# Four layers of a hybrid network in one kernel: where the state-space scan of image 2 in layer 3 stands among the scans of layer 0

## The chip, the cores and the metric

The kernel runs on one core of a Trainium2 chip. TensorE (PE) multiplies matrices into PSUM; VectorE (DVE), ScalarE (ACT) and GpSimd (POOL) work element by element; SyncE (SP) issues almost all transfers. Each engine executes its own instructions in the order in which the program lists them. The metric is device time in microseconds (us) of one execution, the median of several runs.

## The reference, cut to what matters

Four images of 32 x 32 pixels and 256 channels pass four layers. Layer 0 is a convolution block with a selective scan, layer 1 a grouped convolution, layer 2 masked attention and a mixture of eight experts, layer 3 a second selective scan and a second mixture of eight experts. The scans are the only steps that run along the 1024 positions of an image one after the other:

```python
def step(h, inp):                        # layer 0: 512 channels, 64 states each
    xt, dtt, Bt, Ct = inp
    dA = jnp.exp(dtt[:, :, None] * A)
    h = dA * h + (dtt * xt)[:, :, None] * Bt[:, None, :]
    y = jnp.einsum('bdn,bn->bd', h, Ct)
    return (h, y)
...
def scan_step(h, inputs):                # layer 3: 512 channels, 16 states each
    x_t, dt_t, B_t, C_t = inputs
    A_bar = jnp.exp(dt_t[..., None] * A)
    B_bar = dt_t[..., None] * B_t[:, None, :]
    h_new = A_bar * h + B_bar * x_t[..., None]
    y_t = (h_new * C_t[:, None, :]).sum(axis=-1)
    return (h_new, y_t)
```

Everything that an image passes between the scans is per position or per image. The images don't depend on one another.

## The kernel before, in words

**A scan** is written (layer, image): (0, 3) is layer 0's of image 3. Its 512 channels are four blocks d of 128. A block is cut into *units*: a unit is a tile of 128 rows (channel and state) by 1024 positions. Layer 0 has 64 states, so 2 channels to a unit and 64 units to a block; layer 3 has 16 states, so 8 channels to a unit and 16 units to a block. Four scans of 256 and four of 64 units make 1280.

**A unit** (`scans`, L352 to L511) takes these steps. `load` (L419) fetches the step sizes of its channels, each channel's row broadcast over its states: one transfer (L425) per channel, so 2 of 256 KB in layer 0 and 8 of 64 KB in layer 3, all from SP. `decay` (L431) makes exp(dt A) on ACT. `first` (L441) spreads the inputs over the states on PE (`ps_rep`). Then DVE multiplies by B (L499) and runs the recurrence (L503, `TENSOR_TENSOR_SCAN`), POOL multiplies by C (L504), and after every second unit `pair` (L456) sums over the states on PE (`ps_y`); at the end of half a block the sum goes to DRAM (L479). Loads run four units ahead through five buffers, `ps_rep` has two. `chunk` (L372) fetches a block's inputs (`S`) and, with block 0, the scan's B and C (`rows`, two buffers each), 12 units ahead (AHEAD).

**The order of the units** is one list for the whole kernel, written by hand (L31): `SCANS = ((0, 0), (0, 1), (3, 0), (0, 2), (3, 1), (0, 3), (3, 2), (3, 3))`, each scan with all its blocks. Counted through from 0, (3, 1) is units 832 to 895, (0, 3) is 896 to 1151, (3, 2) is 1152 to 1215 and (3, 3) is 1216 to 1279.

**All other work** is twelve *stages* (L33), written as generators that yield between pieces and are laid between the steps of the units. `front` (image b) is layer 0 up to its scan. `middle` (b), L1782, is the rest of layer 0 (`back0`), layer 1, attention, the first experts and layer 3 up to its scan (`front3`); it asks for scan (0, b). `last` (b), L1792, is the rest of layer 3 (`back3`), the second experts and the output; it asks for scan (3, b). One stage is open at a time. `advance` (L526) runs the open stage's next piece. When none is open it takes the first stage in the list whose scan is whole, otherwise the first whose scan has its blocks 0 and 1; a stage that then comes to a block that isn't scanned yet waits, and no other is taken up meanwhile (L537).

**How much is laid beside a unit** is decided before anything runs, by an estimated clock for each engine (`Metered`, L92; `run`, L548): after each half of a unit, up to two pieces are laid down, as long as no engine's clock is ahead of DVE's. Where a scan's inputs aren't made yet by the time that its units are near (5 units, LATEST), `need` (L513) lays down stage pieces one after the other, with no units between them, until they are. Attention that is laid down in that way takes the scan's PSUM buffers for its scores (`ps_sx` in place of `ps_sc`, L1329).

Stages take SBUF from one stack, so a stage's transfers into its tiles wait until the stage before has let go of that memory.

Of the kernel before, what the change touches and what calls it, by code (L numbers as in the profile page):

```python
# [22 lines left out]
DC = DI // P  # L23
# [4 lines left out]
SCATTERS = ((0, 64), (64, 96), (96, 160), (160, 288), (288, 544))  # L28


SCANS = ((0, 0), (0, 1), (3, 0), (0, 2), (3, 1), (0, 3), (3, 2), (3, 3))  # L31

STAGES = (  # L33
    ("front", 0, None), ("front", 1, None), ("front", 2, None), ("front", 3, None), ("middle", 0, (0, 0)),
# [7 lines left out]
AHEAD = 12  # L42
LATEST = 5
# [89 lines left out]
class Hybrid:  # L133
# [182 lines left out]
    def scan_setup(self, stage, psum, name, n):  # L316
# [4 lines left out]
        nc, pool = self.nc, self.const  # L321
        G = P // n
        units = DI // G
        cols = pool.tile([P, units], F32, name="A_" + name)
        flat = self.a[name].rearrange("(u g) n -> u (g n)", g=G)
        for k in range(0, units, P):
# [6 lines left out]
        nc.vector.tensor_scalar(cols, cols, -1.0, None, ALU.mult)  # L333
        spread = pool.tile([3 * 32, 32 // G, P], BF16, name="spread_" + name)
        for s in range(3):
# [4 lines left out]
            )  # L340
        mine = stage.tile([P, G], F32, name="mine_" + name)
        nc.vector.tensor_reduce(
            mine, self.ident.rearrange("p (g n) -> p g n", n=n), AX.X, ALU.add
        )
        collect = pool.tile([P, 32 // G, 32], F32, name="collect_" + name)
        nc.gpsimd.memset(collect, 0.0)
# [4 lines left out]
    def scans(self, mp, psum):  # L351

        nc = self.nc
        units = []  # L360
        for scan in SCANS:
            G = P // self.states[scan[0]]
            units += [
                (scan, d, c, i, j)
                for d in range(DC) for c in range(2) for i in range(32 // G) for j in range(2)
            ]
        chunks, rows, waiting = {}, {}, []
        state = {}
        self.scan_psum = psum
        y = None  # L370

        def chunk(k):  # L372

            if k >= len(units):
                return
            scan, d, c, i, j = units[k]
            if (c, i, j) != (0, 0, 0):
                return
            n = self.states[scan[0]]
            self.need(scan, d)  # L380
            if d == 0:
                bct = self.mem["bc", *scan]
                pair = []
                for t in range(2):
                    x = mp.tile([P, L], F32, tag=f"rows{t}", name=f"rows{t}", bufs=2)
                    for g in range(P // n):
                        nc.sync.dma_start(x[g * n : (g + 1) * n, :], bct[t * n : (t + 1) * n, :])
                    pair.append(x)
                rows[scan] = pair
            S = mp.tile([3 * 32, 4, L], BF16, tag="S", name="S", bufs=2)  # L390
            for s in range(3):
                nc.sync.dma_start(
                    S[32 * s : 32 * s + 32, :, :],
                    self.mem["parts", *scan, d][s].rearrange("(j p) t -> p j t", p=32),
                )
            chunks[scan, d] = S

        def chunks_ahead(k, late=False):

            if not late and k + AHEAD < len(units) and units[k + AHEAD][2:] == (0, 0, 0):
                waiting.append(k + AHEAD)
            while waiting:
                scan, d = units[waiting[0]][:2]
                if ("parts", *scan, d) not in self.ready:
                    if waiting[0] - k > LATEST:
                        break
                    if not late:
                        return True  # L410
                    self.alone = True
                chunk(waiting.pop(0))
                self.alone = False
            return False

        def load(k):
            if k >= len(units):
                return
            scan, d, c, i, j = units[k]  # L419
            n = self.states[scan[0]]  # L420
            G = P // n
            a = mp.tile([P, L], F32, tag="dA", name="dA", bufs=5)
            for g in range(G):
                r = 64 * c + 32 * j + G * i + g
                nc.sync.dma_start(  # L425
                    a[g * n : (g + 1) * n, :],
                    self.mem["dt", *scan, d][r : r + 1, :].to_broadcast([n, L]),
                )
            state[k] = a

        def decay(k):  # L431
            if k >= len(units):
                return
            scan, d, c, i, j = units[k]
            G = P // self.states[scan[0]]
            col = (d * P + 64 * c + 32 * j) // G + i
            nc.scalar.activation(
                state[k], state[k], AF.Exp, scale=self.tables[scan[0]][0][:, col : col + 1]
            )

        def first(k):  # L441
            if k >= len(units):
                return
            scan, d, c, i, j = units[k]
            spread = self.tables[scan[0]][1]
            G = P // self.states[scan[0]]
            ps = psum.tile([P, L], F32, tag="x", name="ps_rep", bufs=2)
            for g in range(2):
                cols = slice(g * 512, (g + 1) * 512)
                nc.tensor.matmul(  # L450
                    ps[:, cols], lhsT=spread[:, i, :], rhs=chunks[scan, d][:, 2 * c + j, cols],
                    start=True, stop=True,
                )
            state[k] = (state[k], ps)

        def pair(k):  # L456

            nonlocal y
            scan, d, c, i, j = units[k]
            n = self.states[scan[0]]  # L460
            per = 32 * n // P
            collect = self.tables[scan[0]][2]
            if i == 0:
                y = psum.tile([P, 512], F32, tag="y", name="ps_y", bufs=1)
            h = [state.pop(k - 1), state.pop(k)]
            for g in range(2):
                for j in range(2):
                    at = 32 * (2 * g + j)
                    nc.tensor.matmul(
                        y[at : at + 32, :], lhsT=collect[:, i, :],  # L470
                        rhs=h[j][:, g * 512 : (g + 1) * 512],
                        start=(i == 0), stop=(i == per - 1), tile_position=(0, at),
                    )
            if i == per - 1:
                yo = mp.tile([P, 512], F32, tag="yo", name="yo", bufs=2)
                nc.scalar.copy(yo, y)
                to = self.keep(("y", *scan, d, c), [64, L])
                for g in range(2):
                    nc.sync.dma_start(to[:, g * 512 : (g + 1) * 512], yo[64 * g : 64 * g + 64, :])  # L479
                if c == 1:  # L480
                    self.done.add((scan, d))

        for k in range(AHEAD):
            chunk(k)
        for k in range(4):
            load(k)
        decay(0)
        decay(1)
        first(0)
        for k in range(len(units) + 4):  # L490
            waits = chunks_ahead(k)
            load(k + 4)
            if not waits:
                first(k + 1)
            decay(k + 2)
            if k < len(units):
                a, inp = state.pop(k)
                B, Cm = rows[units[k][0]]
                nc.vector.tensor_tensor(inp, inp, B, ALU.mult)  # L499
            yield  # L500
            if k < len(units):
                h = mp.tile([P, L], F32, tag="h", name="h", bufs=5)
                nc.vector.tensor_tensor_scan(h, a, inp, 0.0, ALU.mult, ALU.add)  # L503
                nc.gpsimd.tensor_tensor(h, h, Cm, ALU.mult)  # L504
                state[k] = h
            if k % 2 == 1 and 2 <= k < len(units) + 2:
                pair(k - 2)
            if waits:
                chunks_ahead(k, True)
                first(k + 1)  # L510
            yield  # L511
# [1332 lines left out]
```

## Time and profile before

| what | us |
|---|---|
| median of 3 runs (6766.81 to 6776.79) | 6769.17 |
| the profiled execution, by its own time | 6786.48 |
| span of the profiled execution, first to last instruction | 6784.8 |
| DVE busy (77% of the span) | 5227.3 |
| PE busy (79%) | 5361.8 |
| DVE, the recurrence: 1280 instructions, 2285 ns each | 2925.2 |
| DVE, the product with B: 1280 instructions, 1213 ns each | 1552.8 |

All times in what follows are from the span's start. The k-th `TENSOR_TENSOR_SCAN` on DVE is unit k, counted from 0, so the timeline of DVE gives the time of each unit. Those that matter here, by the start of the recurrence:

| unit | what begins there | us |
|---|---|---|
| 1028 | `last` of image 1, beside (0, 3) | 4798.9 |
| 1134 | `last` of image 1 is all laid down | 5236.8 |
| 1152 | (3, 2); with it `middle` of image 3 can go on | 5314.7 |
| 1211 | after it, `need` lays down most of the rest of `middle` of image 3 | 5598.8 |
| 1216 | (3, 3) | 6031.4 |
| 1222 | `last` of image 2, beside (3, 3) | 6060.5 |
| 1279 | the last unit | 6343.7 |

The profile's page has the whole execution's sums; the views by stretch of time, by tile and as a timeline show what happens in one stage. In a timeline a row gives start, length, engine, line, operation, output and inputs, how many instructions are merged, and in brackets the engine's idle time before and what ended it. Most instructions of the scans and stages have the line of the recording helper (L124), so they are told apart by tile.

### The profile page before, as it was taken

To read this page: it belongs to the slowest core of one execution; us is meant where nothing else is said; L and a number is where in the kernel's file an instruction comes from. 1 tells how busy PE (TensorE), PEld (TensorE's weight loads), DVE (VectorE), ACT (ScalarE), POOL (GpSimd) and SP (SyncE) were. 2 spreads that over 40 slices of the span, in tenths; PEclk is the share of its full clock that TensorE was granted. 3 is DMA by queue.
4 is the path that set the end of the run, shared out by engine and by line. 5 is a ranking of instruction groups with operands and counts; after the bars stand their busy time and mean duration, and the time that the engine had idled before them with its cause. 6 is when DMAs were issued, how large, how long until landed. Compare 5 with 4: busy or idle time off the path is not lost. (4 is left out here: it accounts for less than half of the span.)

```text
span 6784.8 us, 65796 instructions
## 1 busy us (share of the span) xinstructions
PE 5361.8 (79%) x20236; PEld 2166.3 (32%) x20320; DVE 5227.3 (77%) x4486; ACT 3447.1 (51%) x4112; POOL 3649.0 (54%) x1801
## 2 busy tenths in 40 slices
PE   6558778679798568979689679898698688967979
PEld 3002213122252022234145232253254222514556
DVE  8778998978798997789889987898899871247411
ACT  2426666445477334557558445476386344245411
POOL 0876786755457665555856655556756551054200
PEclk8559778589798578979789789898699788977989
DMA  2556665754365765446656755456666750146221
GB/s 73 147 144 160 179 171 155 193 133 124 102 164 158 185 162 143 116 117 178 180 148 170 184 149 132 107 140 176 177 167 171 167 133 14 50 130 151 79 62 35
DMA packets 394235, 937.44 MB, mean 138 GB/s; under 512 B 83220, under 2 KB 165728, under 8 KB 392224
## 3 DMA queue, kind: packets, MB, share of 16 engines
q1 hardware_dynamic: 391696, 930.53, 52.1%
q8 instruction: 172, 2.82, 0.2%
q0 software_dynamic: 2128, 2.13, 0.2%
q14 instruction: 239, 1.96, 0.1%
HBM read 842.59 MB, written 93.95 MB: 138 GB/s over the span
## 5 line engine op out<-in xcount | busy, mean ns | idle before, releaser
L124 POOL TENSOR_TENSOR h<-h,rows 128x1024 f32<-128x1024 f32 x1280 | 3031.3, 2371 | 1999.9 <-DVE h L124 1649.9
L124 DVE TENSOR_TENSOR_SCAN h<-dA,ps_rep 128x1024 f32<-128x1024 f32 x1280 | 2925.2, 2285 | 234.0 <-issue 106.0
L124 DVE TENSOR_TENSOR ps_rep<-ps_rep,rows 128x1024 f32<-128x1024 f32 x1280 | 1552.8, 1213 | 287.8 <-PE ps_rep L124 287.3
L124 ACT ACTIVATE dA<-dA,A_L_conv_A_log 128x1024 f32<-128x1024 f32 x1024 | 1154.2, 1145 | 727.6 <-DMA dA<-dt 636.5
L124 PE MATMUL ps_rep<-S,spread_L_conv_A_log 96*128 96x512 bf16 x2048 | 766.7, 465 | 740.7 <-DVE h L124 709.1
L124 PE MATMUL ps_y<-h,collect_L_conv_A_log 128*32 128x512 f32 x4096 | 804.1, 762 | 96.0 <-POOL h L124 94.6
L124 PE MATMUL ps_h<-xTm,we 128*128 128x512 f32 x1536 | 719.4, 608 | 3.4 <-ACT h_m L124 1.8
L124 PE MATMUL ps_e<-we,h_m 128*128 128x256 f32 x3072 | 703.2, 382 | 10.9 <-ACT h_m L124 10.4
L124 ACT ACT_TABLE_LOAD x495 | 635.1, 1283 | 76.2 <-PE ps_h L124 44.4
L124 PEld LDWEIGHTS <-spread_L_conv_A_log 96*128 96x128 bf16 x2048 | 161.6, 103 | 1520.5 <-DVE h L124 1209.6
L124 PEld LDWEIGHTS ps_e<-we,h_m 128*128 128x128 f32 x3072 | 583.3, 191 | 157.2 <-issue 45.4
L124 DVE SCALAR_TENSOR_TENSOR tb<-ps_e,cw,tb 128x256 f32<-128x256 f32 x512 | 220.7, 474 | 415.5 <-PE ps_e L124 415.5
L124 ACT ACTIVATE h_m<-ps_h,cols 128x512 f32<-128x512 f32 x384 | 260.4, 686 | 473.8 <-PE ps_h L124 471.0
L124 ACT ACTIVATE dA<-dA,A_L_attn_A_log 128x1024 f32<-128x1024 f32 x256 | 293.5, 1148 | 390.3 <-DMA dA<-dt 354.0
L124 ACT ACTIVATE p<-ps_sc 128x512 f32<-128x512 f32 x432 | 234.4, 594 | 450.6 <-PE ps_sc L124 295.5
L124 PEld LDWEIGHTS ps_h<-xTm,we 128*128 128x128 f32 x1536 | 292.9, 194 | 341.8 <-issue 295.2
L124 PE MATMUL ps_at<-p,v 128*32 128x512 f32 x1024 | 357.6, 616 | 45.8 <-ACT p L124 35.1
L124 PE MATMUL ps_rep<-S,spread_L_attn_A_log 96*128 96x512 bf16 x512 | 185.4, 451 | 205.8 <-DVE h L124 184.3
L124 PE MATMUL ps_sc<-qT,kT 32*128 32x512 f32 x864 | 251.7, 654 | 42.1 <-ACTq L1248 24.5
L124 PE MATMUL ps_at<-p,ones 128*32 128x512 f32 x1024 | 275.1, 616 | 0.0
L124 PEld LDWEIGHTS ps_y<-h,collect_L_conv_A_log 128*32 128x32 f32 x4096 | 107.9, 120 | 495.9 <-POOL h L124 248.3
L124 PE MATMUL ps_cv<-pad,diag 128*128 128x512 f32 x576 | 260.4, 594 | 0.0
(311 smaller groups left out, 5012.4 us busy)
## 6 DMA issues: line engine op xcount, KB each, us to landing
dA<-dt SPq DMA_DIRECT2D x2048, 256.0 KB
dA<-dt SPq DMA_DIRECT2D x2048, 64.0 KB
we<-in_L_ffn_W_dram SPq DMA_DIRECT2D x64, 512.0 KB
parts<-parts SPq DMA_DIRECT2D x64, 384.0 KB
S<-parts SPq DMA_DIRECT2D x96, 256.0 KB
dt<-sp_r SPq DMA_DIRECT2D x64, 256.0 KB
y<-yo SPq DMA_DIRECT2D x128, 128.0 KB
y_back<-y SPq DMA_DIRECT2D x64, 256.0 KB
```

The lines of the kernel that those rows point to most:

```text
L124: return got(*args, **kw)
```

## The change

`SCANS` becomes a list of scans with ranges of blocks, and may hold a pause:

```diff
-SCANS = ((0, 0), (0, 1), (3, 0), (0, 2), (3, 1), (0, 3), (3, 2), (3, 3))
+SCANS = (
+    ((0, 0), range(DC)), ((0, 1), range(DC)), ((3, 0), range(DC)), ((0, 2), range(DC)),
+    ((3, 1), range(DC)), ((0, 3), range(2)), ((3, 2), range(DC)), ((0, 3), range(2, DC)), None,
+    ((3, 3), range(DC)),
+)
...
         for scan in SCANS:
+            if scan is None:
+                units += [None] * (LATEST + 1)
+                continue
+            scan, blocks = scan
             G = P // self.states[scan[0]]
             units += [
                 (scan, d, c, i, j)
-                for d in range(DC) for c in range(2) for i in range(32 // G) for j in range(2)
+                for d in blocks for c in range(2) for i in range(32 // G) for j in range(2)
             ]
+
+        def some(k):
+            return k < len(units) and units[k] is not None
```

Every step of a unit (`chunk`, `load`, `decay`, `first`, the two products, the recurrence, `pair`) asks `some(k)` instead of `k < len(units)`. So units 0 to 1023 are what they were. Then come (3, 2) whole as units 1024 to 1087, (0, 3) blocks 2 and 3 as 1088 to 1215, six empty places that issue nothing for a unit but in which stages can be advanced, and (3, 3) as places 1222 to 1285.

What the stages do with that follows from `advance`. When `last` of image 1 is laid down, at unit 1134, (3, 2) is whole and (0, 3) isn't; so `last` of image 2 comes next, and `middle` of image 3 after it. In the order of the built kernel's instructions `last` of image 2 begins at unit 1134; by the pause all but its last 22 pieces are laid down; there the inputs of (3, 3) are missing, and `need` lays down those 22 pieces and then `middle` of image 3 up to the first parts of (3, 3), with no unit between them. The units of (3, 3) come next, the first ten of them beside the last pieces of `front3`. `last` of image 3 begins beside them, but its pieces wait for blocks of (3, 3). No instruction of the computation is added or taken away; the attention of image 3 takes its scores in `ps_sx` throughout.

More of the change, by code (lines that the diff above doesn't have):

```diff
@@ L372, in chunk @@
         def chunk(k):
-            if k >= len(units):
+            if not some(k):
                 return
@@ L398, in chunks_ahead @@
         def chunks_ahead(k, late=False):
-            if not late and k + AHEAD < len(units) and units[k + AHEAD][2:] == (0, 0, 0):
+            if not late and some(k + AHEAD) and units[k + AHEAD][2:] == (0, 0, 0):
                 waiting.append(k + AHEAD)
@@ L416, in load @@
         def load(k):
-            if k >= len(units):
+            if not some(k):
                 return
@@ L431, in decay @@
         def decay(k):
-            if k >= len(units):
+            if not some(k):
                 return
@@ L441, in first @@
         def first(k):
-            if k >= len(units):
+            if not some(k):
                 return
@@ L495, in scans @@
             decay(k + 2)
-            if k < len(units):
+            if some(k):
                 a, inp = state.pop(k)
@@ L500, in scans @@
             yield
-            if k < len(units):
+            if some(k):
                 h = mp.tile([P, L], F32, tag="h", name="h", bufs=5)
@@ L505, in scans @@
                 state[k] = h
-            if k % 2 == 1 and 2 <= k < len(units) + 2:
+            if k % 2 == 1 and 2 <= k < len(units) + 2 and some(k - 2):
                 pair(k - 2)
```

## The prediction

> **What bounds the kernel now.** I read the page first. DVE is busy 77% and PE 79%, and which of them holds depends on the stage. The chain that ended last reaches back only some 6% of the span, through PE's expert products, so the end is a stretch with PE alone. That made me cut the last 2000 us by the units' times (front) and ask for the busy time of each stretch: length, then PE, PE's weight loads, DVE, ACT, POOL, then the granted PE clock, the DMA share and GB/s.
>
> ```profile
> 4798.90:5236.80 437.90, 389.09 (x1540) 198.30 (x1540) 403.05 (x325) 298.35 (x290) 265.34 (x119) 0.89 0.63 165
> 5236.80:5314.70 77.90, 37.33 (x108) 4.36 (x108) 67.92 (x39) 19.52 (x17) 47.38 (x23) 0.50 0.89 224
> 5314.70:5598.80 284.10, 220.51 (x961) 82.47 (x969) 229.44 (x186) 122.25 (x160) 158.81 (x74) 0.84 0.58 140
> 5598.80:6014.60 415.80, 361.12 (x1381) 166.44 (x1388) 75.65 (x183) 150.72 (x212) 44.57 (x35) 0.91 0.11 36
> 6014.60:6060.50 45.90, 23.12 (x68) 4.59 (x68) 38.32 (x27) 22.60 (x29) 38.31 (x23) 0.57 0.72 182
> 6060.50:6346.00 285.50, 214.54 (x791) 105.20 (x792) 223.88 (x188) 147.78 (x151) 149.83 (x70) 0.78 0.63 157
> 6346.00:6477.30 131.30, 130.60 (x467) 87.16 (x465) 16.73 (x39) 25.82 (x37) 2.34 (x1) 1.00 0.09 27
> 6477.30:6784.80 307.50, 262.73 (x904) 176.91 (x904) 43.52 (x115) 53.34 (x82) 14.81 (x12) 0.89 0.18 53
> ```
>
> Row 1 is `last` of image 1 beside layer 0's units: both engines near 90%. Row 2 is 18 units with no stage beside them: PE half idle. Rows 3 to 5 are `middle` of image 3, first with the units of (3, 2), then (row 4) with none, then with the first units of (3, 3). Rows 6 and 7 are `last` of image 2, beside (3, 3) and then alone; row 8 is `last` of image 3. So there are three places where one kind of work runs without the other: row 2, row 4 and rows 7 and 8. From (0, 3) on, the order that nothing can cut is (0, 3), `middle` 3, (3, 3), `last` 3; the question is what stands beside it.
>
> Then the same view for tile dA alone, whose DVE count is recurrences, for 57 units from the start of each `last`, first layer 0's, then layer 3's:
>
> ```profile
> 4798.90:5045.00 246.10, 130.25 (x57) 63.37 (x57) 0.80 0.66 170
> 6060.50:6343.60 283.10, 130.25 (x57) 64.06 (x56) 0.77 0.63 156
> ```
>
> A unit takes 4.32 us in the first and 4.97 in the second, beside the same stage work. SP's timeline gives a reason, 48 issues (six units of layer 3) in one go:
>
> ```profile
> 6231.07 23.34 SPq L425 DMA_DIRECT2D dA<-dt  x48
> ```
>
> That is 0.486 us an issue, 3.9 us a unit, where DVE needs 3.60 (starts of recurrences in DVE's timeline, 3929.25, 3932.85, 3936.45).
>
> **The change part by part.** It adds no instruction; it moves what stands beside what. I follow it from unit 1024, with the profiled execution's times.
>
> 1. *Units 1024 to 1087 are (3, 2) in place of block 2 of (0, 3).* The stage work beside them is the same: the end of `middle` 2, then `last` 1 from unit 1028. Each unit now issues 8 transfers on SP in place of 2. By the two rows above, (283.1 - 246.1) x 64/57 = 41.5; I take **+40**. The bounds are 0 (SP at 3.9 us a unit keeps ahead of 4.32) and 42. Its 16 transfers of `rows` only move from before unit 1152 to before 1024, with loads four units ahead as cover; the buffers are free, since they were those of (3, 1).
>
> 2. *`last` 2 begins at unit 1134, beside (0, 3) blocks 2 and 3.* Row 2's **78 us** without a stage are filled: -78. `last` 2 then has 82 units of layer 0 beside it, as `last` 1 had. In `last` 1 the products `ps_e` of expert block 11, the first of the 22 pieces left, started at 5155.4, 356.5 us after unit 1028. The 22 pieces are three blocks of 16 `ps_h` and 32 `ps_e` and two halves; alone such a block takes 13.77 us (`ps_e` starts 6353.17 and 6366.95, in PE's timeline), so 3 x 13.77 + 2 x 6.9 = 55.1. `last` 2 takes 356.5 + 55.1 = 411.6 in place of rows 6 and 7, 416.8: **-5** (bounds -20 and +5).
>
> 3. *`middle` 3 runs with no unit beside it.* From 5314.7 to unit 1222 (rows 3 to 5) it took 745.8.
>  - 5314.7 to 5606.7, the end of its third pair of heads, with 60 units beside it: 292. Alone a pair of heads takes 22.7 (5606.67 to 5629.37 in PE's timeline), beside units 33.9: 3 x 11.2 = 34 saved. The normalisation between `ps_h` and `ps_tr` (5404 to 5429) takes 25, alone 8 to 9 (5897.7 to 5905.3, 7.6): 16. The wait before the first scores (5475 to 5505) takes 30, of which PE's last 11.2 are no unit's: I take 13, 17 saved. `ps_o` of `back0` 23, against 15.9 for 64 at 0.248 us (58 in 14.4 at the end): 7. Other products 6. Lost: the y and u of (0, 3) can only be fetched when `last` 2 lets go of its memory; `last` 3 shows that fetch, 6477.3 to the last block at 6504.9, 27.6, against 15.5 here (5314.7 to 5330.2): -13. Together 67 saved, 225 left.
>  - 5606.7 to 5973.4 is alone already: 366.7, unchanged.
>  - 5973.4 (the step sizes of (3, 3)) to 6060.5, 87: the first unit of (3, 3) now follows at once, without four units of (3, 2) before it (17 us) and six of (3, 3) counted here (29): 87 - 17 - 29 = 41, and I add 7 for the transfers of `rows`, `S` and `dt` of (3, 3), which landed behind those units: 48.
>  So 225 + 367 + 48 = 640, **-106**. Bounds: PE's own work in the first part is 227.9 less 40.9 (`ps_rep`) and 41.5 (`ps_y`), 145.5, and with the fetch some 160, which gives -171; if only the heads get faster, -60.
>
> 4. *(3, 3) has nothing beside it.* `last` 2 is gone, `last` 3 waits for it. What a lone scan costs isn't in the trace; DVE's pace is 3.60, SP's 3.9. SP also issues the stores of y, `S` and the fetches of `last` 3, some 0.3 us a unit, and each fetch of a block waits on SP for that block's store to land (store 6089.91, fetch 6095.40: 4.4 us after the store's issue had ended), with the loads of later units behind it. I take 4.3 us: 63 x 4.3 = **+271**. Bounds: 3.60 (227) and 4.97 (313). The first ten units share ACT and DVE with `front3`'s end, within that.
>
> 5. *`last` 3.* Before, its fetch came after `last` 2 (6477.3 to 6504.9), here three of four blocks are in before the scan ends. After the last recurrence: POOL, `ps_y`, copy 6.6 us (6343.66 to the store at 6350.21), store to fetch 5.5 as above, and some 5 for the load, then as before from the last gating to the end:
>
> ```profile
> 6504.92 2.48 POOL L124 TENSOR_TENSOR y_back<-y_back,gate_back 128x512 f32<-128x512 f32 x2 [1.36 <-DMA y_back<-y]
> 6506.24 14.40 PE L124 MATMUL ps_o<-w_L_attn_W_out,y_back 128*128 128x256 f32 x58 [2.62 <-POOL y_back L124]
> ```
>
>  6784.8 - 6504.9 = 279.9, with 17 before it 297 in place of 307.5: **-11**.
>
> Sum: 40 - 78 - 5 - 106 + 271 - 11 = **+111 us**, or 6897 for the profiled execution (6786.48). The median stands 17 us below that execution, so 6769.2 + 111 = **6880 us**. The change fills 78 us of DVE and buys `middle` 3 a free run; it pays with a whole scan in the open, which before stood under `last` 2.
>
> A rule against the change is in the Trainium skill, "DMA: Bandwidth & Descriptors", section "Measured (HBM→SBUF, 128 partitions, SWDGE, issued from GpSimd)": transfers below 64 KB are dominated by descriptors, and one of 64 KB takes 0.95 us. If the eight of a unit ran one after the other, 7.6 us a unit, an estimate from that page, (3, 3) would take 479 us and the sum would be +319. The trace speaks against it, with recurrences of layer 3 that start 3.8 us apart (3913.31 to 3940.05, seven steps): transfers overlap, and SP's issue is the limit.
>
> **The rivals.**
> - *Slower still.* The round trip of y on SP starves the lone scan (4.97 or more, as in its slowest row), and `middle` 3 is held by its own chain, not by the units (-60): 40 - 78 - 5 - 60 + 313 - 11 = +199, 6968. For it: PE is busy only 145 of 292 us there. Against it: heads are measured alone.
> - *A wash.* SP keeps ahead in (1), the lone scan runs at 3.75 (236) and `middle` 3 gives 145: 0 - 78 - 5 - 145 + 236 - 11 = -3, 6766.
> - *Faster.* The one mechanism is that units laid between a stage's pieces cost `middle` 3 more than their own time. It decides in 5314.7 to 5606.7: with the lone scan at DVE's 3.60 (227) and +40 kept, `middle` 3 must save 187 to be 14 us ahead, 147 with step 1 at nothing; so the first part must fall from 292 to some 144, below the bound of 160, or with the swap free to some 184. At its bound of -171 and the swap free: 0 - 78 - 5 - 171 + 227 - 11 = -38, 6731.
> - That the order isn't changed as said is excluded by the built program.
>
> **How the numbers follow.** Forecast, +50 to +160: 0.78. Slower still: 0.12. Wash: 0.05. Faster: 0.05. A measurement of this kernel tells 0.2%, 13.5 us, from no change. Faster 0.05, the same 0.05, slower 0.90. All bounds together run from -53 (0 - 78 - 20 - 171 + 227 - 11) to +211 (42 - 78 + 5 - 60 + 313 - 11), but they are independent; 8 in 10 lie from about +35 to +190: **6805 to 6960**.
>
> **What would show it.** Right: the 64 last recurrences stand in a stretch of about 270 us with PE mostly idle and a clock of 0.5; no recurrence for some 640 us before it; row 2's gap is gone; heads of 22.7 us all through. Wrong: the lone scan at 3.6 us a unit, step 1 free, or `middle` 3 below 560 us.

## The result and the profile after

| | before | after |
|---|---|---|
| median, both measured side by side (us) | 6772.98 (6766.81 to 6788.31) | 6871.71 (6861.00 to 6884.43) |
| the profiled execution (us) | 6786.48 | 6884.43 |
| its span (us) | 6784.8 | 6882.7 |
| PE's mean granted clock | 0.827 | 0.822 |

The change makes the kernel slower by 98.7 us, a ratio of 1.0143 with a 95% interval of 1.0118 to 1.0168. 6880 was forecast. The two spans lie 97.9 us apart, so the profiles can be cut against each other.

The page's sums hide it: PE is busy 5402.2 us in place of 5361.8, DVE 5222.2 in place of 5227.3. As before I read by stretches. The view is the busy time of stretches, for the kernel after, with the columns of the prediction's first table. The rows are `last` 1, `last` 2, `middle` 3 in three parts (to the end of its third pair of heads, to the step sizes of (3, 3), to the first unit of (3, 3)), the scan (3, 3), and `last` 3:

```profile
4813.97:5288.80 474.83, 394.69 (x1540) 201.36 (x1540) 403.78 (x326) 302.77 (x296) 265.45 (x119) 0.87 0.60 163
5288.80:5701.20 412.40, 363.85 (x1400) 192.85 (x1400) 321.02 (x274) 236.11 (x237) 208.25 (x95) 0.90 0.53 140
5701.20:5894.50 193.30, 149.73 (x655) 64.88 (x655) 32.60 (x71) 54.60 (x73) 21.98 (x18) 0.87 0.18 57
5894.50:6261.20 366.70, 329.29 (x1293) 153.46 (x1289) 64.92 (x170) 114.47 (x158) 18.77 (x15) 0.91 0.09 29
6261.20:6311.29 50.09, 28.50 (x61) 11.35 (x60) 8.82 (x12) 37.59 (x54) 27.24 (x22) 0.84 0.36 107
6311.29:6589.55 278.26, 130.47 (x380) 17.58 (x380) 219.55 (x131) 83.10 (x82) 168.89 (x81) 0.52 0.58 162
6589.55:6882.70 293.15, 265.22 (x912) 177.31 (x912) 45.04 (x114) 55.25 (x84) 8.45 (x6) 0.91 0.12 35
```

The row of 78 us without a stage is gone. In its place stands the sixth row: 278 us in which PE is busy for 130 and has a clock of 0.52. Between the start of the last unit of layer 0 (5640.0) and that of the first unit of (3, 3) lie 671 us, where the prediction's sign was some 640 without a recurrence: besides the 610 us of `middle` 3 they hold the last 61 of `last` 2, which the prediction had among its terms but not in that sign. Of the 610, DVE is busy for 106. `last` 1 beside its units takes 474.8 us, where before it took 437.9: that is the swap itself.

The same view for tile dA alone. The first row is the 57 units from unit 1028, most of them layer 3's now; the second is the scan (3, 3), 63 intervals:

```profile
4813.97:5097.40 283.43, 130.25 (x57) 64.02 (x56) 0.78 0.60 162
6311.29:6589.55 278.26, 144.04 (x63) 72.22 (x63) 0.52 0.58 162
```

283.4 us for 57 units is 4.97 each, to the hundredth the pace that layer 3's units had beside `last` before (283.1). Alone they take 4.42.

The end of the kernel, in the timeline, answers to the last lines of the prediction: the last gating comes 14 us after the start of the last recurrence (6589.55), where the prediction had 17, and with the products that follow it the rest runs as before.

```profile
6603.45 2.48 POOL L129 TENSOR_TENSOR y_back<-y_back,gate_back 128x512 f32<-128x512 f32 x2 [6.68 <-issue]
6604.77 15.12 PE L129 MATMUL ps_o<-w_L_attn_W_out,y_back 128*128 128x256 f32 x58 [5.61 <-POOL y_back L129]
```

Put beside the prediction's steps, from the same units or products in both profiles:

| step | predicted (us) | measured (us) |
|---|---|---|
| up to unit 1024 (same instructions) | 0 | 4798.4 - 4783.3 = +15.1 |
| 1: units 1024 to 1134 | +40 | 490.4 - 453.5 = +36.9 |
| 2: row 2 gone; `last` 2 | -78; -5 | -77.9; 412.4 - 416.8 = -4.4 |
| 3: `middle` 3 | -106 | 610.1 - 745.8 = -135.7 |
| 4: the scan (3, 3) alone | +271 | +278.3 |
| 5: `last` 3 | -11 | 293.15 - 307.50 = -14.4 |
| sum | +111 | +97.9 |

### The profile page after: what moved, and what is told of

Its sections match the earlier page's. It is cut to its first block, busy times and chain, and to the rows that moved or that the text cites. A ratio compares the mean times of both kernels' runs of the same rounds, so it can differ in the third digit from the quotient of the medians.

```text
span 6882.7 us, 65921 instructions
## 1 busy us (share of the span) xinstructions
PE 5402.2 (78%) x20320; PEld 2159.4 (31%) x20320; DVE 5222.2 (76%) x4486; ACT 3490.3 (51%) x4120; POOL 3648.7 (53%) x1801
## 5 line engine op out<-in xcount | busy, mean ns | idle before, releaser
L129 PE MATMUL ps_rep<-S,spread_L_attn_A_log 96*128 96x512 bf16 x512 | 204.4, 492 | 284.9 <-DVE h L129 259.7
L129 ACT ACTIVATE p<-ps_sc 128x512 f32<-128x512 f32 x384 | 208.3, 594 | 406.1 <-PE ps_sc L129 401.6
L129 PEld LDWEIGHTS ps_h<-xTm,we 128*128 128x128 f32 x1536 | 291.9, 194 | 344.9 <-issue 294.1
L129 PE MATMUL ps_sc<-qT,kT 32*128 32x512 f32 x768 | 223.8, 654 | 31.7 <-DMA dA<-dt 13.8
```

Of the source, the lines that this page charges most:

```text
L129: return got(*args, **kw)
```

## The experiments

Two things were to be tested: whether the change is slow for the reason given (a scan left in the open, worth more than `middle` 3's free run), and whether layer 3's pace, on which steps 1 and 4 rest, comes from SP's issues. The rival for the second was that the transfers land late for a reason of their own (their size, the rows they read, the DMA engines' load), or that ACT's queue holds the exps back.

The stretches of every run, from its profile, in us, each from the start of its first recurrence to the start of the first recurrence behind it; (3, 3) stands last and is counted as 63 intervals. In the kernels with the order before, and in e3, (3, 3) stands beside `last` 2. e3, e5, e8 and e9 were timed once, the others four times or more:

| kernel | time (us) | (3, 0) | (3, 1) | 1024-1087 | (3, 3) |
|---|---|---|---|---|---|
| before | 6773-6786 | 304.5 | 305.1 | 273.4 (layer 0) | 312.3 |
| after | 6871.7 | 308.2 | 307.8 | 310.6 | 278.3 |
| e1 after, one load of eight rows | 6932.6 | 338.1 | 330.4 | 320.9 | 264.3 |
| e2 before, the same load | 6869.6 | 334.3 | 333.7 | 274.6 (layer 0) | 320.9 |
| e3 after, `last` 2 behind `middle` 3 | 6943.1 | 307.5 | 305.9 | 311.1 | 305.9 |
| e4 before, pause | 6792.7 | 308.0 | 305.5 | 275.4 (layer 0) | 310.2 |
| e5 after, one load of one row | 6751.5 | 291.0 | 290.6 | 272.7 | 233.2 |
| e6 after, loads five ahead | 6830.7 | 296.1 | 299.2 | 307.1 | 277.2 |
| e7 after, late copy | 6881.8 | 311.9 | 315.8 | 308.6 | 279.3 |
| e8 after, y fetched from ACT | 6877.6 | 310.0 | 308.8 | 312.0 | 278.8 |
| e9 after, eight loads of one row | 6877.0 | 307.6 | 306.5 | 311.6 | 277.4 |
| e10 after, state by state | 6764.4 | 291.8 | 289.4 | 273.6 | 242.1 |
| e11 before, state by state | 6693.4 | 291.9 | 290.9 | 274.3 (layer 0) | 271.6 |
| e12 before, state by state, five ahead | 6697.0 | 290.2 | 290.3 | 274.3 (layer 0) | 271.0 |

### The order's own parts: e3 and e4

e3 lets `last` 2 open only after `middle` 3:

```diff
             can = [
                 x for d in (DC - 1, EARLY) for x in self.todo
-                if x[2] is None or (x[2], d) in self.done
+                if (x[2] is None or (x[2], d) in self.done)
+                and (x[:2] != ("last", 2) or all(z[0] != "middle" for z in self.todo))
             ]
```

> The changed order of units, but the stage last of image 2 may not open before middle of image 3 has: it then stands beside (3, 3) again, and units 1134 to 1215 have nothing beside them. Theory (what counts is which units have a stage beside them): 82 bare units of layer 0 at 3.9 us, 320 in place of 351; middle of image 3 as short as in the changed kernel; (3, 3) and last of image 2 together about 417 in place of 278 and 61 alone; in all 60 to 80 slower than the changed kernel, 6930 to 6960. Rival (stage work and units add up whatever their order, so only the place of (3, 2) counts): within 20 of 6872.

Measured: 6943.1 us, 71 above the changed kernel. The view is the busy time of stretches for this kernel: units 1134 to 1151, units 1152 to 1215, the time to the first unit of (3, 3), the scan (3, 3):

```profile
5284.00:5354.75 70.75, 37.31 (x108) 4.35 (x108) 64.66 (x38) 19.52 (x17) 47.33 (x23) 0.51 0.83 217
5354.75:5583.28 228.53, 125.33 (x380) 14.78 (x380) 216.05 (x128) 70.94 (x63) 149.14 (x64) 0.50 0.55 145
5583.28:6182.28 599.00, 507.94 (x1993) 228.87 (x2009) 103.90 (x250) 208.43 (x287) 67.43 (x53) 0.90 0.11 35
6182.28:6488.19 305.91, 214.91 (x775) 96.78 (x776) 245.00 (x201) 153.76 (x161) 174.57 (x85) 0.74 0.64 163
```

Now layer 0's last 82 units are bare (70.8 + 228.5 us, PE's clock 0.50) and (3, 3) stands under `last` 2 again, in 306 us. With (3, 2) moved ahead there is one `last` for two stretches, these 82 units and (3, 3): beside whichever it stands, the other is bare. That `last` 2 fills the gap in the changed kernel is part of what the change earns, as step 2 has it.

e4 has the order before, written in the new form, with the pause of six empty places ahead of (3, 3):

```diff
+SCANS = tuple(
+    (x, range(DC)) for x in ((0, 0), (0, 1), (3, 0), (0, 2), (3, 1), (0, 3), (3, 2))
+) + (None, ((3, 3), range(DC)))
```

> The order of the kernel before, with the six empty places ahead of (3, 3) and nothing else changed. Theory (the pause itself costs nothing): within 15 us of 6773; middle of image 3 has all 64 units of (3, 2) beside it in place of 60, and last of image 2 opens ten units into (3, 3) in place of six. Rival (the pause is a part of the loss, since no unit stands ready when the inputs of (3, 3) are made): 25 to 50 slower.

Measured: 6792.68 us, ratio to before 1.0015 (1.0003 to 1.0026). That is 8 us in a loss of 99: the pause is not what costs.

### One transfer in place of eight, and why it was slow: e1, e2, e5, e9

e1 and e2 load a unit of layer 3 with one transfer of 512 KB:

```diff
+            r = 64 * c + 32 * j + G * i
+            if scan[0] == 3:
                 nc.sync.dma_start(
...
+                    a,
+                    self.mem["dt", *scan, d][r : r + G, :].unsqueeze(1).to_broadcast([G, n, L]),
+                )
```

> The changed kernel, with the eight loads of a unit of layer 3 (64 KB each, one per channel) written as one transfer of 512 KB with the same rows. Theory (SP's issues set the pace of layer 3's units): the lone scan (3, 3), 278 us for 63 steps in the changed kernel, falls to 3.6 to 3.7 us a unit, about 230; units 1024 to 1134, 490 us there, fall by about 35 to the 454 of the kernel before; the other three scans of layer 3 gain 10 to 30 each; in all 90 to 150 us faster than the changed kernel, 6720 to 6780. Rival (the chain of landing, exp, recurrence and freed buffer sets the pace, or the bytes do): the lone scan stays at 4.2 to 4.5 us a unit or gets slower, and the time stays within 20 us of 6872.

> The kernel before with the same one load for a unit of layer 3. Theory (SP's issues): its layer-3 scans, 4.76 to 4.97 us a unit beside stages, come near the 4.1 to 4.3 of layer 0's units, 30 to 40 us for each of four: 6640 to 6690. The changed order stays slower than this by 40 to 100, because its scan (3, 3) still has nothing beside it. Rival (chain or bytes): 6773, no change.

Measured: e1 6932.6 us, 1.0222 of before (1.0202 to 1.0243), slower than the change itself; e2 6869.55, 1.0126 (1.0107 to 1.0145). Both expectations of the "issue" theory fell, and so did the rival's, by which the time would stay where it was. Only the lone scan gained (264.3, its undisturbed intervals 3.54 us), and beside stages all got worse. I had changed two things at once, as the next two runs were made to show. e5 loads one row, broadcast to all 128 partitions, in one transfer; e9 keeps eight transfers but lets all read one row:

```diff
+                r = 64 * c + 32 * j + G * i                              # e5
+                nc.sync.dma_start(a, self.mem["dt", *scan, d][r : r + 1, :].to_broadcast([P, L]))
...
-                r = 64 * c + 32 * j + G * i + g                          # e9
+                r = 64 * c + 32 * j + G * i + (g if G == 2 else 0)
```

> The changed kernel, but a unit of layer 3 loads one channel's row broadcast to all 128 rows in one transfer of 512 KB, in place of eight transfers of 64 KB from eight rows (the other seven channels' step sizes are left out, so those values are not the reference's). SP issues one instruction a unit, the bytes written are the same. Theory 'SP's issue is the limit': the lone scan of (3, 3) falls from 278 to about 240 us, units 1024 to 1087 from 311 to about 280, the whole from 6872 to 6760-6800. Theory 'a transfer of 512 KB lands as one piece and therefore later than eight of 64 KB': like the merged load from eight rows, 320 us for units 1024 to 1087, about 264 for the lone scan, 6920-6940 in all. Theory 'eight source rows in one transfer were what slowed the merged load': units 1024 to 1087 at or below 311, 6840-6870.

> The changed kernel with its eight transfers of 64 KB a unit of layer 3, but all eight read the same row (seven channels' step sizes are left out, so those values are not the reference's). It stands between the changed kernel (eight issues, eight rows) and the load of one row in one transfer (6751). Theory 'the eight issues a unit on SP': as the changed kernel, 308-313 us for units 1024 to 1087, 274-282 for the lone scan, 6865-6890 in all. Theory 'reading eight rows of DRAM': as the single row, 273 and 233, about 6750.

Measured: e5 6751.46 us, a little below what the "issue" theory had; e9 6877.04, as that theory had it. The busy time of units 1024 to 1087 in the kernel after (its lone scan is in the first table of this part):

```profile
4798.36:5108.99 310.63, 230.60 (x844) 108.37 (x845) 247.29 (x203) 162.31 (x167) 170.74 (x82) 0.78 0.61 167
```

The same two stretches (units 1024 to 1087, then (3, 3) alone), first e1, then e9, then e5:

```profile
4841.75:5162.65 320.90, 235.04 (x844) 108.55 (x845) 245.78 (x204) 161.02 (x166) 170.80 (x82) 0.75 0.65 159
6372.49:6636.74 264.25, 131.03 (x380) 17.28 (x380) 219.52 (x131) 83.12 (x82) 169.29 (x81) 0.51 0.60 170
```

```profile
4795.09:5106.67 311.58, 230.84 (x844) 109.15 (x845) 247.29 (x203) 162.41 (x167) 170.59 (x82) 0.77 0.67 166
6304.12:6581.56 277.44, 130.58 (x380) 17.58 (x380) 219.54 (x131) 83.09 (x82) 169.04 (x81) 0.52 0.64 163
```

```profile
4742.60:5015.31 272.71, 223.93 (x844) 106.81 (x845) 246.88 (x204) 162.46 (x168) 170.86 (x82) 0.82 0.62 189
6222.80:6456.05 233.25, 130.25 (x380) 17.25 (x380) 221.06 (x132) 82.08 (x82) 169.33 (x81) 0.51 0.59 191
```

All three do the same work on DVE, ACT and POOL (busy times within 2 us of each other). e9 is the changed kernel again: eight reads of one row are as slow as reads of eight rows. e5 is faster than the changed kernel by 38 and 45 us, and than e9, which reads the same one row, by 39 and 44: the number of transfers decides, not the rows they read. What then held e1? The trace also records every packet of the DMA engines. I counted how many were under way at once in units 1024 to 1087, as shares of the stretch:

| packets under way | after | e1 | e5 | e10 (below) |
|---|---|---|---|---|
| none | 13% | 4% | 26% | 19% |
| exactly 8 | 4% | 46% | 2% | 1% |
| 16 | 16% | 12% | 23% | 35% |

In e1 eight packets are under way for 46% of the stretch, and for 65% of a quiet piece of its lone scan: the transfer whose outermost count is 8 keeps eight at a time going. This agrees with the Trainium skill: "DMA: Bandwidth & Descriptors", section "Rules for kernel authors", has it that the engines of a transfer follow from the slowest dimension of its access patterns, so that one of fewer than 16 keeps the transfer to that many engines. The same section advises to merge many small transfers into one large; e1 shows that this alone can lose.

SP is not what is late in e1. The view is who SP waited for in units 1024 to 1087; the columns are us in total, times, the longest. This row is its wait for a buffer that DVE still reads:

```profile
SPq L437 <- DVE h L129: 96.5, 25, 9.6
```

The starts of the instructions say which end is late. Medians over the units of the lone scan (3, 3), in us:

| | after | e9 | e1 | e5 | e10 (below) |
|---|---|---|---|---|---|
| from the unit's last load issue on SP to its recurrence | 3.9 | 4.0 | 15.4 | 15.4 | 15.4 |
| from that issue to the unit's exp on ACT | 2.5 | 2.6 | 11.7 | 4.9 | 6.6 |

With eight transfers (after, e9) the loads land soon but are issued late. With one transfer SP issues early; in e1 the load then lands late, in e5 and e10 it doesn't.

### One transfer with 16 outermost: e10, e11, e12

So layer 3's units were laid out state by state: partition = 8 x state + channel. Tables, B, C and the sums over states are built to match; the transfer then repeats eight rows 16 times, with 16 outermost:

```diff
+            if n == 16:
+                r = 64 * c + 32 * j + G * i
+                eight = self.mem["dt", *scan, d][r : r + G, :].unsqueeze(0).to_broadcast([n, G, L])
+                nc.sync.dma_start(a, eight)
...
+        by_state = self.ident.rearrange("p (s g) -> p g s", g=G)
         nc.vector.tensor_reduce(
-            mine, self.ident.rearrange("p (g n) -> p g n", n=n), AX.X, ALU.add
+            mine, by_state if n == 16 else self.ident.rearrange("p (g n) -> p g n", n=n), AX.X, ALU.add
```

> The changed kernel with layer 3's units laid out state by state in place of channel by channel (partition = 8 x state + channel; the tables, B and C rows are built to match). One transfer of 512 KB then reads the eight rows with 16 as its outermost count in place of 8; B and C rows of layer 3 take one transfer each in place of eight. Theory 'the merged load was slow because only eight packets were in flight at a time': 16 in flight, units 1024 to 1087 in 270-278 us (310.6), the lone scan in 232-240 (278), 6740-6770 in all. Theory 'eight source rows in one transfer are slow': as the first merged load, 315-325 and 260-265, 6910-6940.

> The kernel before with the same layout and the same single transfer. If the load's form is what makes layer 3's units slow: (3, 0) and (3, 1) in 290-293 us (305), (3, 3) in 273-282 (312), 6705-6735 in all; the change of order, with this load, is then worth +10 to +50 us in place of +99, since its first step costs nothing and its lone scan 45 us less. If not: as the merged load in the kernel before, 6860-6880.

Measured: e10 6764.41 us, 0.9966 of before (0.9952 to 0.9980); e11 6693.37, 0.9868 (0.9851 to 0.9884). Busy time of the two stretches for e10:

```profile
4755.54:5029.12 273.58, 221.42 (x844) 103.27 (x845) 246.62 (x203) 162.67 (x168) 170.30 (x81) 0.81 0.75 188
6231.07:6473.17 242.10, 129.39 (x380) 17.59 (x380) 219.73 (x132) 82.79 (x82) 168.81 (x81) 0.53 0.77 185
```

Same rows, same bytes, the DMA engines even busier than after the change (0.75 against 0.61 of the stretch), and yet 273.6 in place of 310.6 us and 242.1 in place of 278.3. So it is neither the size of a transfer nor the rows that it reads nor the load on the DMA engines that makes layer 3's units late. SP's own waits for a free buffer tell what changed, in the same view and stretch as for e1. First the kernel before (layer 0's units there), then after, then e10:

```profile
SPq L425 <- DVE h L124: 125.3, 47, 8.0
```

```profile
SPq L437 <- DVE h L129: 14.2, 9, 2.8
```

```profile
SPq L456 <- DVE h L129: 107.9, 37, 8.3
```

As long as SP has these waits it is ahead, and its issues set no pace; e1's 96.5 us show that the landings may still do so. Beside layer 0's units SP waits 125 us of 273; beside layer 3's eight transfers 14 of 311; beside one transfer 108 of 274.

e11 is the faster version of the two orders by 71 us (6764.4 - 6693.4). I had expected 10 to 50. The stretches show what I left out. With the quick load the change's first step costs nothing (e10 takes 453.0 us from unit 1024 to 1134, e11 454.1) and the lone scan 36 us less; but the order before gets its own share: `last` 2, which has (3, 3) beside it there, takes 380.0 us, counted to the end of its last product (416.7 before), where in the changed order it has layer 0's units beside it and stays at 413.6 (412.4 without the quick load); and `middle` 3, which has (3, 2) beside its first part there, takes 723.2 us up to unit 1222 (745.8 before). The view is the busy time of stretches for e11: units 1134 to 1151, the stretch with (3, 2) and most of `middle` 3, (3, 3) from its first unit, and the rest:

```profile
5202.55:5278.46 75.91, 37.33 (x108) 4.37 (x108) 67.18 (x39) 19.82 (x18) 47.29 (x23) 0.50 0.90 230
5278.46:5973.09 694.63, 587.85 (x2387) 249.77 (x2387) 317.38 (x376) 280.64 (x384) 216.25 (x118) 0.89 0.32 84
...
5976.54:6248.12 271.58, 220.59 (x820) 103.17 (x824) 245.45 (x202) 156.58 (x163) 172.82 (x82) 0.77 0.70 180
6248.12:6689.93 441.81, 395.40 (x1380) 264.67 (x1372) 62.58 (x155) 79.79 (x120) 17.14 (x13) 0.92 0.15 46
```

The first row, 76 us without a stage, is still there: the gap that the change fills.

e12 adds to e11 the deeper loads of e6:

> The kernel before with the state-major layout, and loads five units ahead through six buffers. If the deeper loads help layer 0's units as well as layer 3's (in the changed kernel the four stretches of layer 0 before unit 1024 were some 20 us shorter in all): 6675-6705, 20-35 below the state-major layout alone. If they helped only by hiding the eight issues of layer 3: within 8 us of the state-major layout alone.

Measured: 6696.95 us, 0.9876 of before (0.9860 to 0.9893), within 4 us of e11. In the order before, deeper loads gain nothing once the eight issues are gone.

### Rivals for layer 3's pace: e6, e7, e8

e6 loads five units ahead, through six buffers:

```diff
-            a = mp.tile([P, L], F32, tag="dA", name="dA", bufs=5)
+            a = mp.tile([P, L], F32, tag="dA", name="dA", bufs=6)
...
-            load(k + 4)
+            load(k + 5)
```

> The changed kernel with loads five units ahead through six buffers in place of four through five (the pause is two places longer, so that the order closes). The number of issues and the bytes stay. Theory 'late landings' (step sizes that land after ACT wants them, with SP held back by the buffers): ACT's wait for dA falls by half or more, units 1024 to 1087 fall from 311 to 285-297, the lone scan from 278 to 255-268, the whole from 6872 to 6800-6845. Theory 'SP's issue count': nothing changes in those stretches by more than 5 us, the whole stays within 6855-6890.

Measured: 6830.67 us, 1.0077 of before (1.0060 to 1.0094), so 41 us below the change and, as a whole, where the "late landings" theory had it. The two stretches are where the "issue count" theory had them: units 1024 to 1087 fell by 3.5 us and the lone scan by 1.1. The gain lies elsewhere: (3, 0) and (3, 1) fell by 12 and 9 and layer 0's stretches before unit 1024 by some 27 in all. SP's wait for a free buffer in units 1024 to 1087, and ACT's wait for the step sizes there:

```profile
SPq L437 <- DVE h L129: 12.1, 14, 2.5
```

```profile
ACT dA L129 <- DMA dA<-dt: 82.8, 21, 9.4
```

Both are as in the kernel after (14.2 and 81.5). In the lone scan SP waits for a buffer for 1.6 us in the kernel after, and the sixth buffer lets it issue no earlier (4.1 us before the recurrence for 3.9). In (3, 0) it does: 16.1 us for 12.3, and ACT's wait fell from 75.4 to 42.6, although SP's waits for a buffer are short there too (17.7 us in the kernel after). There the trace looks as the "late landings" theory has it; why SP gets further ahead in (3, 0) and (3, 1) is open. Why layer 0's stretches fell is open too: e7 and e5, with five buffers, also had some of them 10 to 17 us shorter than the profile after.

e7 writes the copy of `ps_y` and its stores one unit later:

```diff
             if i == per - 1:
-                yo = mp.tile([P, 512], F32, tag="yo", name="yo", bufs=2)
-                nc.scalar.copy(yo, y)
...
+                flushes.append((y, scan, d, c))
...
             decay(k + 2)
+            if flushes:
+                flush()
```

> The changed kernel with the copy of ps_y to SBUF, and its two stores, written one unit later on ACT and SP (the pause is two places longer). Theory 'ACT's queue waits for ps_y behind POOL and PE, and the exps behind it come late': the 13 us that ACT waits for ps_y between units 1024 and 1088 are gone, that stretch falls from 311 to about 300, the lone scan by some 5 to 273, the whole to 6830-6855. Theories by which loads or SP decide: no stretch changes by over 5 us and the whole stays within 6860-6885; the tail after the last recurrence may be a few us longer.

Measured: 6881.79 us, 1.0153 of before (1.0136 to 1.0170), no gain. The view is ACT's waits in units 1024 to 1087, first after, then e7:

```profile
ACT dA L129 <- DMA dA<-dt: 81.5, 27, 7.2
ACT yo L129 <- PE ps_y L129: 13.3, 3, 7.9
```

```profile
ACT dA L129 <- DMA dA<-dt: 86.1, 25, 9.5
...
ACT yo L129 <- PE ps_y L129: 4.0, 2, 2.7
```

ACT's wait for `ps_y` fell by 9 us, its wait for the step sizes rose by 5, and the stretch lost 2: a wait taken away ahead of the one that ends last only moves there.

e8 issues the y fetches of (3, 3) from ACT:

```diff
-            self.nc.sync.dma_start(y[64 * c : 64 * c + 64, d, :], self.mem["y", *key, d, c])
+            at = self.nc.scalar if key == (3, 3) else self.nc.sync
+            at.dma_start(y[64 * c : 64 * c + 64, d, :], self.mem["y", *key, d, c])
```

> The changed kernel with the fetches of y of (3, 3) by the last stage issued from ACT in place of SP. Theory 'each fetch waits on SP for the store of its block to land, with the loads of the units behind it': the slow intervals of the lone scan around the second and third fetch go, and it takes 260-268 us in place of 278. Theory 'it is the traffic and the other fetches of that stage (its gates, weights)': 275-281. If ACT's own wait at the fetch holds the exps back instead: above 281.

Measured: 6877.58 us, the lone scan 278.8. The slow intervals at the fetches did not go; the longest is 12.7 us in e8 and 9.7 after. ACT's own wait could have put back what SP gained, but SP's waits in the kernel after leave nothing to gain. This row is its wait for the store at the fetches, from 6363 us to the end of the lone scan:

```profile
SPq L794 <- DMA y<-yo: 1.2, 1, 1.2
```

The round trip of y on SP, which the prediction counted among what slows the lone scan, costs 1.2 us.

## Why the prediction was right, step by step

**The answer and its main reason hold.** A scan of 64 units was taken out from beside `last` 2 and left in the open at 278 us; a gap of 78 and a free run of 136 don't pay for that. e3 moves the bare stretch from (3, 3) to layer 0's units and is slower still by 71 us, within the 60 to 80 expected from the same terms.

**Step 1 (+40, measured +36.9)** took the right rows and the right cause. e9, e5 and e10 show that it is the number of transfers: with one transfer and 16 packets under way layer 3's units cost no more than layer 0's (273.6 against 274.3 in e11). One thing I had too simple: it isn't an even pace. Most units of the stretch kept the intervals of before, and the loss sits in some eight long ones (9.9 in place of 3.6 us, 10.5 in place of 6.8, 9.6 in place of 4.1), the early ones beside the fetches of `back3`. An SP with nothing in hand passes such fetches on to the units; that reading rests on where the long ones stand, and no run takes the fetches away.

**Step 2 (-83, measured -82.3)** and **step 5 (-11, measured -14.4)** went as worked out.

**Step 3 (-106, measured -135.7) is the term that was mis-sized**, all in its first part: 193.3 us in place of 225. The 366.7 came out to the tenth, and the end took 50.1 for 48. In the first part the normalisation was right (8.4 us for 8 to 9) and the heads nearly (72.4 us for 68.1, the first pair 27.0). "Other products 6" was the failed piece: they saved some 25, of which layer 1's alone 13 (25.6 us for the 39 that they took with units between them). The wait before the first scores took 3.8 us for 13, and up to the end of `ps_o` 2 us were saved where I had 6 lost (48.6 us against 50.5; the first product came 17.5 us after `last` 2, for 15.5 before, where I had put the fetch at 27.6). Together that is the 32 us. That the whole missed by 13 only is in part luck: 15 us before unit 1024, which no step accounts for, and 7 in step 4 stood against it. The five steps alone sum to +82.8 us, 28 below the forecast.

**Step 4 (+271, measured +278.3)** had the right cause and nearly the right size. SP's timeline in the lone scan, kernel after:

```profile
6371.13 27.46 SPq L437 DMA_DIRECT2D dA<-dt  x56
6408.87 23.08 SPq L437 DMA_DIRECT2D dA<-dt  x48
6433.25 29.94 SPq L437 DMA_DIRECT2D dA<-dt  x64
6463.29 1.09 SPq L491 DMA_DIRECT2D y<-yo  x2
6464.42 0.60 SPq L1732 DMA_DIRECT2D tb<-t  x1
6465.07 0.45 SPq L1737 DMA_DIRECT2D gate_back<-gate  x1
6465.61 6.45 SPq L437 DMA_DIRECT2D dA<-dt  x8
```

It issues without a break, 29.94 / 8 = 3.74 us a unit (3.9 in the prediction), more than the 3.54 that DVE needs with one transfer (e10, e5). On DVE the longest wait from 6371 to 6460, 7.1 us from recurrence to recurrence, looks like this:

```profile
6412.93 1.21 DVE L129 TENSOR_TENSOR ps_rep<-ps_rep,rows 128x1024 f32<-128x1024 f32 x1
6417.79 2.29 DVE L129 TENSOR_TENSOR_SCAN h<-dA,ps_rep 128x1024 f32<-128x1024 f32 x1 [3.66 <-DMA dA<-dt]
```

The excess of the scan over DVE's pace, 63 x 3.54 = 223, is 55 us. By the intervals some 17 of it are three long ones beside `front3`'s end (13.1, 6.5, 8.0), some 16 three beside the fetches of `last` 3 (8.9, 8.0, 9.7), and of the remaining 22 half lie in three more (7.1, 8.0, 6.5), the rest scattered over many short ones. With one issue a unit (e10) 19 of the 55 are left, beside `front3` and the fetches. The part of step 4 that named the round trip of y is refuted: SP waits 1.2 us for it.

**The rule weighed against the change** (transfers of 64 KB one after the other, 7.6 us a unit) stays refuted: alone a unit with its eight transfers takes 4.42.

**What stays open.** That the loads are issued late on SP, and not landed late, is shown for the lone scan (3.9 us before the recurrence against 15.4); beside `last` 1, in units 1024 to 1087, the medians go the same way (10.4 against 17.2 in e5). What the price of an issue consists of isn't: eight take 3.74 us in a free run, but 6.45 at 6465.61, among the fetches, and whether SP itself or the queue behind it takes that time, no run here tells apart. The 15.1 us before unit 1024 stay open too. Five kernels execute the same instructions up to there and reach it at 4774.6 (e4), 4783.3 (before), 4791.5 (e8), 4793.2 (e3) and 4798.4 (after), one profile each: a spread of 24, but the three with the changed order are the later ones.

## What to carry to other kernels

Ask of each moved step what it leaves bare: (3, 3) alone cost its whole 278 us, while `last` 2 took hardly less time beside layer 0's units (412.4) than it had beside (3, 3) and alone (416.8). Look at what the issuing queue waits for: long waits for free buffers mean that its issues don't set the pace, though late landings still may (e1). Where these waits are gone, ask how long before its use a load is issued, and how long it takes to land; the two call for different remedies. Merge transfers only in a form that still keeps all 16 packets under way: the merge lost 61 us with 8 outermost and gained 107 with 16 (there with the rows of B and C merged too).

## What the hardware did that I had not expected

- One transfer of 512 KB with 8 as its outermost count was slower than eight of 64 KB (e1, 6932.6 against 6871.7 us), with 8 packets under way for 46% of a stretch; with 16 outermost it was faster (6764.4).
- Eight transfers that read one row took as long as eight that read eight rows (311.6 and 310.6 us), though a packet of 4096 bytes took 265 ns on average in the one and 236 in the other.
- DVE's shortest regular step of a unit is 3.54 us where a unit's step sizes come in one transfer, 3.60 where they come in eight, or in layer 0's two; in the first the timeline shows no idle time ahead of the recurrence, in the second 0.19 us, mostly with nothing named that it waited for. First the kernel after, then e10, in their lone scans:

```profile
6424.99 2.29 DVE L129 TENSOR_TENSOR_SCAN h<-dA,ps_rep 128x1024 f32<-128x1024 f32 x1 [0.19 <-issue]
```

```profile
6285.90 2.29 DVE L129 TENSOR_TENSOR_SCAN h<-dA,ps_rep 128x1024 f32<-128x1024 f32 x1
```
